# Grouping value sums by three, differencing sorted values where they are sorted, and moving six small operations to GpSimd in a graph network kernel

## The chip, the cores and the metric

The kernel runs on one core of a Trainium2 chip. The metric is the device time of one execution in microseconds (us), the median of several runs. A difference counts if it is larger than about 0.2 per cent.

## What is computed

The input is 16 graphs of N = 1024 nodes with C = 64 features, a dense adjacency matrix for each, and a node mask. Four layers follow one another, each with a residual and a layer norm. Nearly all of the work is in the first layer, cut here to what matters:

```
adj_d = dilate(adj, mask)            # per node: m neighbours; if m > 10, remove every
                                     # ceil(m/2)-th neighbour, then make it symmetric
sv   = sort(x[neighbours of i])      # per node i and channel c
agg  = 0.25*q(0.25) + 0.5*q(0.5) + 0.25*q(0.75)    # quantiles, each interpolated
                                     # between two order statistics, lo and hi
y    = (relu((x + agg) @ W1 + b1) @ W2 + b2) * mask
```

Three quantiles with two order statistics each make S = 6 statistics. The other layers are three graph convolutions with the adjacency, one with a degree norm, and one weighted mean.

## The kernel before

The kernel does not sort per node. It sorts each channel of a graph once over all 1024 nodes (`sort_pair`, two graphs at a time, 128 rows of 1024 values), and then finds, for every node, the block of the sorted order in which its order statistic lies by counting neighbours with matmuls. The sort is a bitonic network on VectorE (called `V`, DVE in the profile) of 55 steps; what was swapped is written to device memory (`swaps`) and read back in 55 further steps that carry ranks back to the original order (tiles `sr`). Sorted values are in 64 blocks of F = 16.

The value of an order statistic is a sum of differences of sorted values, taken with matmuls, so the kernel needs second differences along the sorted order, split in two fp16 parts, in a tile `txw` with the block index on the partitions. Before the change `sort_pair` writes the sorted values in fp32 to device memory (`xs`, L404: 4 DMAs for each pair of graphs, runs of 16 values), and `steps_of` (L463 to L494), once for each graph, reads them back block by block (L476, L477), forms the differences on VectorE (tile `xc`), and writes `txw`, with zeros in the lanes of the other channel of a pair (factors `PEVEN`, `PODD`).

The main loop works on units: a graph, a group of channels (8 for each graph) and a half of the nodes, 16 units for each graph and 256 in all. Each unit has 6 places y, one for each statistic s, so there are 1536 values of y. At each y the program issues, with a lag: `words` (matmuls to `pw`), `ranks` (`pr_`), `steps` (`pv`, which reads `mt` and `txw`, then ScalarE's eviction to `val`) and `sums` (`fc`), then on VectorE `masks` for statistic y + 1 (a comparison `mt` and a product `pr`), and the counting matmuls `x` of the next unit, whose results ScalarE (`A`, ACT in the profile) evicts to `cc` and `dw`.

`sums` takes the fp32 tiles `val` of two statistics at every second place and multiplies each by the constant `fin`. Each result has 32 rows, and the statistic number modulo 3 selects the group of 32 columns of the array and of 32 partitions of the bank `fc`:

```
for i in (s - 1, s):
    g3, second = i % 3, i // 3
```

Work for other graphs is put between: the sort of the next pair, the dilation of the next graph (`dilate`), the degrees, and the last three layers of the graph before (`layers`). They are Python generators; a class `Spread` steps them at places (two places for each y) so that they are spread evenly to a due place, and holds them back where a simple count of VectorE's work (2.9 us allowed for each place) says that it is behind. A generator may ask for a pause: `yield "4"` is at least four places. All orders are fixed when the program is built: each engine runs its own instructions in that order, and nearly every DMA is issued by SyncE's queue (SP), also in order. Tiles come from pools with a fixed number of buffers; `mt` has four, `pr` two, `cc` and `dw` two, `val` three, and the sort's tiles (tag `s`, names `sv`, `sr`, `ii`) two. `layers` calls a power on GpSimd (POOL) for `rstd` (L774), the only GpSimd work in the loop beside the index ramp `ii` (L412).

In `dilate`, for each of 8 row tiles t of a graph, VectorE makes a running count (`TENSOR_TENSOR_SCAN`) and then six operations on one number for each node (tile `sk`, L532 to L539); after a pause ScalarE uses them as a bias (L543), and VectorE goes on.

Ahead of the loop the first pair is sorted and the first graph dilated, one dilation step for every four sort steps (L1096).

Of the kernel before, what the change touches and what calls it, by code (L numbers as in the profile page):

```python
# [10 lines left out]
F32 = mybir.dt.float32  # L11
F16 = mybir.dt.float16
# [5 lines left out]
ALU = mybir.AluOpType  # L18
AX = mybir.AxisListType

P = 128
T_THRESH = 10.0

MAGIC = 1.5 * 2.0**23
EPS = 1e-5

TURN = 2
# [10 lines left out]
def gnn_stack(  # L38
# [220 lines left out]
    nc.sync.dma_start(out=mask8, in_=maskT)  # L259


    rows_in = [dram1.tile([5, C, N], F16, name=f"rows{i}") for i in range(2 * TURN)]


# [94 lines left out]
    def sort_pair(b, rows, found):  # L359
# [33 lines left out]
        V.tensor_scalar(  # L393
            scaled, v, lo, bits[:, 1:2].bitcast(F32), ALU.subtract, ALU.mult
        )
        v = scaled
        back = dram.tile([P, 2], F32, name="back")
        nc.sync.dma_start(out=back, in_=t[:, 0:2])
        xs = dram.tile([TURN, C // 2, P, F], F32, name="xs")
        for u in range(TURN):  # L400
            for c2 in range(2):
                q0 = (u * 2 + c2) * (C // 2)

                nc.sync.dma_start(  # L404
                    out=xs[u].rearrange("q (b c) f -> c q b f", c=2)[c2],
                    in_=v[q0 : q0 + C // 2, :].rearrange("q (b f) -> q b f", f=F),
                )
        found.append((xs, back))
        yield
        ii, _, _ = slot("ii")  # L410
# [49 lines left out]
                in_=rows.rearrange("y (c q) n -> q y c n", c=2)[KC * gr + k],  # L460
            )

    def steps_of(xs, back, found):  # L463

        least = small.tile([P, 2], F32, tag="least", name="least", bufs=3)
        txw = graph.tile([P, C // 2, 2, 2, F], F16, tag="txw", name="txw", bufs=2)
        found.update(least=least, txw=txw)  # L470
        for h in range(2):
            nc.sync.dma_start(out=least[h * C : (h + 1) * C], in_=back)
        xc = dil.tile([P, 2 * N], F16, tag="d", name="xc").bitcast(F32)
        cur = xc[:, 0:512].rearrange("p (q f) -> p q f", f=F)
        prev = xc[:, 512:1024].rearrange("p (q f) -> p q f", f=F)
        nc.sync.dma_start(out=cur, in_=xs.rearrange("q p f -> p q f"))  # L476
        nc.sync.dma_start(out=prev[2:P], in_=xs[:, 0 : P - 2, :].rearrange("q p f -> p q f"))  # L477
        yield
        V.tensor_copy(prev[0:2], cur[0:2, :, 0:1].to_broadcast([2, C // 2, F]))
        V.tensor_tensor(cur, cur, prev, ALU.subtract)  # L480
        yield

        tx = prev
        V.tensor_tensor(tx[:, :, 0 : F - 1], cur[:, :, 1:F], cur[:, :, 0 : F - 1], ALU.subtract)
        V.tensor_copy(tx[:, :, F - 1 : F], cur[:, :, 0:1])
        part = xc[:, 0:256].bitcast(F16).rearrange("p (q f) -> p q f", f=F)
        yield
        for i in range(2):
            V.tensor_copy(part, tx)
            V.tensor_scalar(txw[:, :, i, 0, :], part, PEVEN, None, ALU.mult)  # L490
            V.tensor_scalar(txw[:, :, i, 1, :], part, PODD, None, ALU.mult)
            if i < 1:
                V.tensor_tensor(tx, tx, part, ALU.subtract)
            yield  # L494


    def dilate(g, found):

# [14 lines left out]
        for t in range(T):  # L513
            sc = dil.tile([P, 2 * N], F16, tag="d", name="sc")
            nb, cum = sc[:, 0:N], sc[:, N : 2 * N]
            q = vt[:, t, :]
            for h in range(2):
                V.tensor_scalar(nb[:, ts(h, HALF)], a[h], 0.0, None, ALU.is_gt)
                A.activation(
                    q[:, ts(h, HALF)], a[h], AF.Copy, accum_out=den[:, h, t : t + 1]  # L520
                )
            if t + 1 < T:
                a = block_of(t + 1)
            V.tensor_tensor(nb[:, ts(t, P)], nb[:, ts(t, P)], offdiag, ALU.mult)

            V.tensor_tensor_scan(cum, nb, nb, 0.0, ALU.add, ALU.max)
            yield
            m = cum[:, N - 1 : N]


            sk = small.tile([P, 5], F32, tag="sk", name="sk")
            V.tensor_scalar(sk[:, 0:1], m, 0.5, 0.5, ALU.add, ALU.mult)  # L532
            V.tensor_scalar(sk[:, 0:1], sk[:, 0:1], MAGIC, -MAGIC, ALU.add, ALU.add)
            V.tensor_scalar(sk[:, 1:2], m, T_THRESH, mk[:, t : t + 1], ALU.is_gt, ALU.mult)
            V.scalar_tensor_tensor(
                sk[:, 2:3], sk[:, 0:1], 1.0, sk[:, 1:2], ALU.add, ALU.mult
            )
            V.tensor_scalar(sk[:, 3:4], sk[:, 2:3], -1.5, 1.5, ALU.mult, ALU.add)
            V.tensor_scalar(sk[:, 4:5], sk[:, 2:3], 0.5, -0.5, ALU.mult, ALU.add)  # L539
            yield "4"  # L540

            for h in range(2):
                A.activation(  # L543
                    q[:, ts(h, HALF)], cum[:, ts(h, HALF)], AF.Abs, bias=sk[:, 3:4]
                )
                yield "2"
            V.tensor_scalar(q, q, sk[:, 4:5], 0.25, ALU.is_equal, ALU.max)
            V.tensor_tensor(q, q, nb, ALU.mult)
            V.scalar_tensor_tensor(
                q[:, ts(t, P)], ident16, 0.25, q[:, ts(t, P)], ALU.mult, ALU.add  # L550
            )
            yield
# [117 lines left out]
    class Unit:  # L670
# [43 lines left out]
        def steps(self, s):  # L714

            pv, mt, nt = bank(ps_e, "pv"), self.mt.pop(s), self.nt.pop(s)
            for i in range(2):
                for k, o in quarters(pv):
                    mm(o, self.gi["txw"][:, KC * self.gr + k, i], mt[:, k], i == 0, False, k)
            for k, o in quarters(pv):  # L720
                mm(o, nbig[:, 32 * k : 32 * k + 32], nt, False, True, k)
            val = work.tile([P, HALF], F32, tag="val", name="val", bufs=3)
            A.activation(val, pv, AF.Relu)
            self.val[s] = val

        def sums(self, s):

            if s == 1:
                self.fc = bank(ps_f, "fc")
            for i in (s - 1, s):  # L730
                g3, second = i % 3, i // 3
                f0 = 16 - 16 * second
                mm(
                    self.fc[32 * g3 : 32 * g3 + 32], fin[:, f0 : f0 + 32], self.val.pop(i),
                    not second, bool(second), g3,
                )

        def weigh(self):
# [237 lines left out]
    def sort_of(i, found):  # L976
        return sort_pair(i * TURN, [rows_of(i * TURN + u) for u in range(TURN)], found)

    def all_of(gen):
        for _ in gen:  # L980
            pass
# [71 lines left out]

    def info(g):


        vt, rd, wd, den = parts.pop()
        infos[g] = dict(vt=vt, rd=rd, wd=wd, den=den, rB={})
        xs, back = sorted_[g // TURN]
        u = g % TURN  # L1060
        return steps_of(xs[u], back[u * C : (u + 1) * C], infos[g])

    def units():
        for g in range(B):
# [25 lines left out]
    for i, _ in enumerate(sorting):  # L1090
        if i == 0:
            onerow = strm.tile([P, N], F32, tag="a", name="onerow").bitcast(F16)[0:C, 0:N]
            V.memset(onerow, 1.0)
            for r in rows_in:
                nc.sync.dma_start(out=r[4], in_=onerow)
        if i % 4 == 3:  # L1096
            next(dilating, None)
    load_rows(rows_of(0), 0)
    load_rows(rows_of(0), 1)
# [7 lines left out]
                word_end(words[0][k], part // 2)  # L1107
            next(dilating, None)
    all_of(dilating)
    stepping = info(0)  # L1110
    next(stepping)
    for s in range(S):
        load_rank(0, s)

# [23 lines left out]
    _, counting = unit_of(0)  # L1138
    all_of(counting)
    live[0].masks(0)  # L1140
    all_of(stepping)

# [40 lines left out]
    for y in range(n_units * S + S):  # L1185
# [4 lines left out]
        if running and z == 0:  # L1190
            infos[g]["aggd"] = dram.tile([C, N], F32, name="aggd")
            deg = small.tile([P, 3, T], F32, tag="deg", name="deg")
            base = 2 * SLOTS * g
            if g == 0 and TURN < B:
                background.append(
                    Spread(sort_of(1, sorted_), 2 * n_sort + 6, 0, base + 2 * SLOTS + ROWS)
                )
            if g + 1 < B:
                background.append(Spread(dilate(g + 1, parts), 64, base, base + 168))
            background.append(  # L1200
                Spread(degrees(g, deg), 2 * T + 2, base, base + 184)
            )
            infos[g]["deg"] = deg
# [3 lines left out]
            if 0 <= v < n_units:  # L1207
                getattr(live[v], what)(s)
        v, s = divmod(y - 4, S)
        if 0 <= v < n_units and s % 2:  # L1210
            live[v].sums(s)
        v, s = divmod(y - 6, S)
        if 0 <= v < n_units and s == S - 1 and all_units[v][2]:
# [19 lines left out]
        for half in range(2):  # L1233

            if running:
# [3 lines left out]
                if g % TURN and place == base + ROWS and g + 3 < B:  # L1239

                    background.append(
                        Spread(
                            sort_of((g + 3) // TURN, sorted_), 2 * n_sort + 6, place,
                            place + 4 * SLOTS,
                        )
                    )
# [1 line left out]
                for b in sorted(background, key=lambda b: -b.late(place)):  # L1248
                    b.at(place)
                if z == 84 and half and g + 1 < B:  # L1250
                    background.append(Spread(info(g + 1), 6, place + 1, base + 2 * SLOTS - 2))
            if running:
                words_at(2 * y + half)
            if nu < n_units:
# [66 lines left out]
```

## Time and profile before

| quantity | value |
|---|---|
| runs, median of 3 (lowest to highest) | 9365.63 us (9364.59 to 9366.08) |
| profiled execution, time | 9361.04 us |
| profiled execution, span | 9359.3 us |
| mean granted TensorE clock | 0.994 |
| TensorE busy | 8767.8 us |
| VectorE busy | 8314.5 us |
| ScalarE busy | 7189.3 us |
| GpSimd busy | 232.7 us |
| first `mt` of the loop starts | about 344 us |
| last matmul of `fc` | about 9220 us |

Busy time is the union of the spans of an engine's instructions. In the groups of the profile each line names the code line, the engine, the operation, out<-in by the program's names and the count; after the bar stand busy time and the mean of one in ns; after the second bar the idle time of the engine just before, and what ended it. L278 and L297 are helpers that record every matmul and every operation of VectorE and ScalarE, so groups are told apart by their tiles.

### The profile page before, as it was taken

Reading aid. Unit: us, or ns where it says so; the run is one execution under the profiler, and the core shown is the slowest. Engines: PE = TensorE matmul, PEld = TensorE weight load, DVE = VectorE, ACT = ScalarE, POOL = GpSimd, SP = SyncE. Lnnn points to the kernel's source line nnn. Section 1 sums busy time; section 2 is a strip of 40 time slices with the busy share of each in tenths; the row PEclk is TensorE's granted clock in tenths of the full one; section 3 lists DMA queues with packets and bytes.
Section 4 is the critical chain, followed back from the end, with each engine's and each line's share of the span. In section 5 each row is a group of like instructions: output and inputs, shape, how many; then the busy total and the mean of one; then the engine's idle time right before and its main releaser. Section 6 shows DMA issues by size and latency. Waiting matters only on the chain.

```text
span 9359.3 us, 188142 instructions
## 1 busy us (share of the span) xinstructions
PE 8767.8 (94%) x78785; PEld 3749.0 (40%) x78785; DVE 8314.5 (89%) x9681; ACT 7189.3 (77%) x12465; POOL 232.7 (2%) x155
## 2 busy tenths in 40 slices
PE   0699999999999999999999999999999999999997
PEld 0334444444444444444444444444444444444442
DVE  8799989999899998989899998999989999777663
ACT  0588878788787887878788787887878788787773
POOL 0000000000000000000000000000000000000000
PEclk9999999999999999999999999999999999999998
DMA  3111221222222222222222222222222222212111
GB/s 84 51 40 42 77 91 61 87 65 90 77 77 73 77 71 80 85 81 67 80 63 89 80 76 81 69 75 77 91 76 75 72 76 74 69 65 66 43 60 57
DMA packets 593540, 676.21 MB, mean 72 GB/s; under 512 B 298736, under 2 KB 413552, under 8 KB 592688
## 3 DMA queue, kind: packets, MB, share of 16 engines
q1 hardware_dynamic: 592688, 664.19, 22.6%
q8 instruction: 616, 10.09, 0.4%
q14 instruction: 236, 1.93, 0.1%
HBM read 584.29 MB, written 79.70 MB: 71 GB/s over the span
## 4 chain that ended last, share of the span: by engine, by line
PE 67%; DVE 20%; ACT 7%; issue 5%; DMA 1%; POOL 0%; SPq 0%; DVEq 0%; POOLq 0%; ACTq 0%
PE x L278 29%; PE pw L278 10%; PE pa L278 10%; PE pv L278 7%; DVE pr L297 5%; PE fc L278 5%; DVE mt L297 4%; DVE sv L297 2%; DVE sr L297 2%; ACT dw L297 2%; DVE vt L297 1%; DVE m L297 1%; PE pc L278 1%; ACT xw L297 1%; PE p L278 1%
## 5 line engine op out<-in xcount | busy, mean ns | idle before, releaser
L278 PE MATMUL x<-vt,xw 128*128 128x512 f16 x16384 | 3974.0, 380 | 91.8 <-ACT dw L297 73.8
L297 DVE TENSOR_TENSOR pr<-mt,dw 128x4096 f16<-128x4096 f16 x1536 | 3520.4, 2292 | 71.8 <-ACT dw L297 1.0
L297 DVE TENSOR_TENSOR mt<-cc,rB 128x2048 f16<-128x2048 f16 x1536 | 1871.8, 1219 | 667.7 <-PE pv L278 646.0
L278 PEld LDWEIGHTS <-xw 128*128 128x128 f16 x16384 | 1497.3, 98 | 1767.8 <-issue 450.5
L297 ACT ACTIVATE qq<-pw,col,icol 128x512 f16<-128x512 f32 x1536 | 1203.0, 783 | 783.0 <-PE pw L278 768.1
L297 ACT ACTIVATE xw<-pa 128x512 f16<-128x512 f32 x2048 | 1234.6, 603 | 450.5 <-PE pa L278 442.8
L297 ACT ACTIVATE dw<-x 128x512 f16<-128x512 f32 x2048 | 1115.8, 600 | 273.7 <-PE x L278 269.3
L278 PE MATMUL pa<-words_by,prow 128*128 128x128 f16 x8192 | 804.3, 221 | 313.7 <-DMA prow<-rows 272.3
L297 ACT ACTIVATE xw<-xw 128x1024 f16<-128x1024 f16 x1024 | 1085.3, 1060 | 11.2
L278 PEld LDWEIGHTS <-prow 128*128 128x128 f16 x8192 | 557.0, 98 | 1159.2 <-issue 961.0
L278 PE MATMUL pw<-pr,red 128*32 128x512 f16 x12288 | 930.4, 379 | 33.1 <-DVE pr L297 32.6
L297 ACT ACTIVATE val<-pv 128x512 f32<-128x512 f32 x1536 | 926.5, 603 | 6.8 <-PE x L278 3.3
L278 PE MATMUL pv<-mt,txw 128*32 128x512 f16 x12288 | 930.6, 379 | 0.2 <-ACT nt L297 0.2
L278 PE MATMUL fc<-val,fin 128*32 128x512 f32 x3072 | 789.0, 592 | 0.5 <-ACT val L297 0.5
L297 ACT ACTIVATE cc<-x 128x512 f16<-128x512 f32 x1024 | 610.3, 596 | 131.4 <-PE x L278 125.9
L297 DVE TENSOR_TENSOR sr<-sr 128x512 f16<-128x512 f16 x1336 | 600.4, 478 | 17.5
L278 PE MATMUL pw<-rB,subr 128*32 128x512 f16 x6144 | 615.6, 390 | 0.2
L278 PE MATMUL pv<-nt,nbig 128*32 128x512 f16 x6144 | 598.7, 379 | 0.0
L297 DVE TENSOR_TENSOR sv<-sv 128x512 f32<-128x512 f32 x880 | 566.7, 685 | 0.0
L278 PEld LDWEIGHTS <-txw 128*32 128x32 f16 x12288 | 330.0, 97 | 334.4 <-issue 1.9
L278 PEld LDWEIGHTS <-subr 128*32 128x32 f16 x6144 | 158.2, 92 | 676.3 <-issue 674.2
L774 POOL TENSOR_TENSOR rstd<-var,neghalf 128x8 f32<-128x8 f32 x112 | 222.2, 1984 | 8112.3 <-DVE var L297 8112.3
(3287 smaller groups left out, 7718.4 us busy)
## 6 DMA issues: line engine op xcount, KB each, us to landing
a<-adj_dram SPq DMA_DIRECT2D x360, 512.0 KB
a<-adjT_dram SPq DMA_DIRECT2D x240, 512.0 KB
da<-adj_dram SPq DMA_DIRECT2D x256, 256.0 KB
ac<-adjT_dram SPq DMA_DIRECT2D x256, 256.0 KB
swaps<-m SPq DMA_DIRECT2D x440, 128.0 KB
m<-swaps SPq DMA_DIRECT2D x440, 128.0 KB
rB<-rd SPq DMA_DIRECT2D x96, 256.0 KB
prow<-rows SPq DMA_DIRECT2D x512, 20.0 KB
```

The source lines that it names most:

```text
L278: link("PE", nc.tensor.matmul(*args, **kw))
L297: ins = call(*args, **kw)
L774: nc.gpsimd.tensor_tensor(rstd, var, neghalf, ALU.pow)
```

## The change

There are three parts, and what follows from them.

**Sums.** `sums` runs at every third statistic, for three statistics at once, one in each of the three column groups. `val` gets a fourth buffer.

**Differences.** `sort_pair` forms the second differences itself, in the sort's own layout (first the difference from the same position of the block before, F values back, then that of neighbours); it splits them in two fp16 parts in the tile `both` and writes them with 8 DMAs for each pair of graphs, runs of 16 fp16 values, to `steps_in`, two buffers in device memory that were filled with zeros at the start. `steps_of` goes; `info` issues one DMA that reads a graph's `txw` whole, and the two for `least`. The sort has two more yields, and its due count is raised by two.

**Node figures.** The six operations on `sk` are issued on GpSimd, and one of them is now a `tensor_scalar` of two scalar operands.

Ahead of the loop, the dilation steps go between the second 55 steps of the first sort, one for every two.

```
+    steps_in = [dram1.tile([TURN, P, C // 2, 2, 2, F], F16, name=f"steps{i}") for i in range(2)]
...
-        xs = dram.tile([TURN, C // 2, P, F], F32, name="xs")
+        yield
+
+        down, _, _ = slot("sv")
+        V.tensor_copy(down[:, 0:F], scaled[:, 0:F])
+        V.tensor_tensor(down[:, F:N], scaled[:, F:N], scaled[:, 0 : N - F], ALU.subtract)
+        step, _, _ = slot("sv")
+        V.tensor_tensor(step[:, 0 : N - 1], down[:, 1:N], down[:, 0 : N - 1], ALU.subtract)
+        firsts, lasts = (a.rearrange("p (b f) -> p b f", f=F) for a in (down, step))
+        V.tensor_copy(lasts[:, :, F - 1 : F], firsts[:, :, 0:1])
+        yield
+        both = sorts.tile([P, 2 * N], F16, tag="s", name="sv")
+        V.tensor_copy(both[:, 0:N], step)
+        V.tensor_tensor(both[:, N : 2 * N], step, both[:, 0:N], ALU.subtract)
+        xs = steps_in[b // TURN % 2]
         for u in range(TURN):
             for c2 in range(2):
                 q0 = (u * 2 + c2) * (C // 2)
-                nc.sync.dma_start(
-                    out=xs[u].rearrange("q (b c) f -> c q b f", c=2)[c2],
-                    in_=v[q0 : q0 + C // 2, :].rearrange("q (b f) -> q b f", f=F),
-                )
+                for i in range(2):
+                    nc.sync.dma_start(
+                        out=xs[u].rearrange("(b e) q i c f -> e i c q b f", e=2)[c2, i, c2],
+                        in_=both[q0 : q0 + C // 2, ts(i, N)].rearrange("q (b f) -> q b f", f=F),
+                    )
...
-    def steps_of(xs, back, found):
...
             sk = small.tile([P, 5], F32, tag="sk", name="sk")
-            V.tensor_scalar(sk[:, 0:1], m, 0.5, 0.5, ALU.add, ALU.mult)
...
-            V.scalar_tensor_tensor(
-                sk[:, 2:3], sk[:, 0:1], 1.0, sk[:, 1:2], ALU.add, ALU.mult
-            )
...
+            G = nc.gpsimd
+            G.tensor_scalar(sk[:, 0:1], m, 0.5, 0.5, ALU.add, ALU.mult)
+            G.tensor_scalar(sk[:, 0:1], sk[:, 0:1], MAGIC, -MAGIC, ALU.add, ALU.add)
+            G.tensor_scalar(sk[:, 1:2], m, T_THRESH, mk[:, t : t + 1], ALU.is_gt, ALU.mult)
+            G.tensor_scalar(sk[:, 2:3], sk[:, 0:1], 1.0, sk[:, 1:2], ALU.add, ALU.mult)
+            G.tensor_scalar(sk[:, 3:4], sk[:, 2:3], -1.5, 1.5, ALU.mult, ALU.add)
+            G.tensor_scalar(sk[:, 4:5], sk[:, 2:3], 0.5, -0.5, ALU.mult, ALU.add)
...
-            val = work.tile([P, HALF], F32, tag="val", name="val", bufs=3)
+            val = work.tile([P, HALF], F32, tag="val", name="val", bufs=4)
...
-            if s == 1:
+            if s == 2:
                 self.fc = bank(ps_f, "fc")
-            for i in (s - 1, s):
-                g3, second = i % 3, i // 3
-                f0 = 16 - 16 * second
+            second = s // 3
+            f0 = 16 - 16 * second
+            for g3 in range(3):
                 mm(
-                    self.fc[32 * g3 : 32 * g3 + 32], fin[:, f0 : f0 + 32], self.val.pop(i),
-                    not second, bool(second), g3,
+                    self.fc[32 * g3 : 32 * g3 + 32], fin[:, f0 : f0 + 32],
+                    self.val.pop(3 * second + g3), not second, bool(second), g3,
                 )
...
+        least = small.tile([P, 2], F32, tag="least", name="least", bufs=3)
+        for h in range(2):
+            nc.sync.dma_start(out=least[h * C : (h + 1) * C], in_=back[u * C : (u + 1) * C])
+        txw = graph.tile([P, C // 2, 2, 2, F], F16, tag="txw", name="txw", bufs=2)
+        nc.sync.dma_start(
+            out=txw.rearrange("p q i c f -> p (q i c f)"),
+            in_=xs[u].rearrange("p q i c f -> p (q i c f)"),
+        )
...
+            nothing = strm.tile([P, N], F32, tag="a", name="nothing").bitcast(F16)
+            V.memset(nothing, 0.0)
+            for r in steps_in:
+                for u in range(TURN):
+                    nc.sync.dma_start(
+                        out=r[u].rearrange("p q i c f -> p (q i c f)"), in_=nothing
+                    )
-        if i % 4 == 3:
+        if i > n_sort and i % 2:
             next(dilating, None)
...
-    stepping = info(0)
-    next(stepping)
+    info(0)
...
-    all_of(stepping)
...
-        if 0 <= v < n_units and s % 2:
+        if 0 <= v < n_units and s % 3 == 2:
             live[v].sums(s)
...
-                    background.append(Spread(info(g + 1), 6, place + 1, base + 2 * SLOTS - 2))
+                    info(g + 1)
```

More of the change, by code (lines that the diff above doesn't have):

```diff
@@ L395, in sort_pair @@
         )
-        v = scaled
         back = dram.tile([P, 2], F32, name="back")
         nc.sync.dma_start(out=back, in_=t[:, 0:2])
-        xs = dram.tile([TURN, C // 2, P, F], F32, name="xs")
+        yield
[11 more added lines that the diff above has]
+        xs = steps_in[b // TURN % 2]
         for u in range(TURN):
@@ L461, in load_rows @@
             )
-    def steps_of(xs, back, found):
[L468 to L494, printed above, removed]
     def dilate(g, found):
@@ L531, in dilate @@
             sk = small.tile([P, 5], F32, tag="sk", name="sk")
-            V.tensor_scalar(sk[:, 0:1], m, 0.5, 0.5, ALU.add, ALU.mult)
-            V.tensor_scalar(sk[:, 0:1], sk[:, 0:1], MAGIC, -MAGIC, ALU.add, ALU.add)
-            V.tensor_scalar(sk[:, 1:2], m, T_THRESH, mk[:, t : t + 1], ALU.is_gt, ALU.mult)
-            V.scalar_tensor_tensor(
-                sk[:, 2:3], sk[:, 0:1], 1.0, sk[:, 1:2], ALU.add, ALU.mult
-            )
-            V.tensor_scalar(sk[:, 3:4], sk[:, 2:3], -1.5, 1.5, ALU.mult, ALU.add)
-            V.tensor_scalar(sk[:, 4:5], sk[:, 2:3], 0.5, -0.5, ALU.mult, ALU.add)
+            G = nc.gpsimd
[5 more added lines that the diff above has]
+            G.tensor_scalar(sk[:, 4:5], sk[:, 2:3], 0.5, -0.5, ALU.mult, ALU.add)
             yield "4"
@@ L1060, in info @@
         u = g % TURN
-        return steps_of(xs[u], back[u * C : (u + 1) * C], infos[g])
+        least = small.tile([P, 2], F32, tag="least", name="least", bufs=3)
[6 more added lines that the diff above has]
+        )
+        infos[g].update(least=least, txw=txw)
     def units():
@@ L1195, in gnn_stack @@
                 background.append(
-                    Spread(sort_of(1, sorted_), 2 * n_sort + 6, 0, base + 2 * SLOTS + ROWS)
+                    Spread(sort_of(1, sorted_), 2 * n_sort + 8, 0, base + 2 * SLOTS + ROWS)
                 )
@@ L1242, in gnn_stack @@
                         Spread(
-                            sort_of((g + 3) // TURN, sorted_), 2 * n_sort + 6, place,
+                            sort_of((g + 3) // TURN, sorted_), 2 * n_sort + 8, place,
                             place + 4 * SLOTS,
```

## The prediction

> **What bounds the kernel now.** I read the engines' shares first, then the chain that ended last, then the groups, then a table of stretches. The first two, from the page:
>
> ```profile
> PE 8767.8 (94%) x78785; PEld 3749.0 (40%) x78785; DVE 8314.5 (89%) x9681; ACT 7189.3 (77%) x12465; POOL 232.7 (2%) x155
> PE 67%; DVE 20%; ACT 7%; issue 5%; DMA 1%; POOL 0%; SPq 0%; DVEq 0%; POOLq 0%; ACTq 0%
> ```
>
> TensorE and VectorE are both nearly full and the chain passes from one to the other. The groups say how they are tied:
>
> ```profile
> L297 DVE TENSOR_TENSOR mt<-cc,rB 128x2048 f16<-128x2048 f16 x1536 | 1871.8, 1219 | 667.7 <-PE pv L278 646.0
> ...
> L278 PE MATMUL fc<-val,fin 128*32 128x512 f32 x3072 | 789.0, 592 | 0.5 <-ACT val L297 0.5
> ```
>
> VectorE waits almost only for `pv`, that is for one of the four `mt` buffers to come free: where it waits, TensorE is the bound. Which one binds where is seen in one graph, cut into eight stretches of 12 places (columns: window, its length, busy us of each engine, clock, DMA):
>
> ```profile
> 2547.00:2610.00 63.00, 61.76 (x588) 25.73 (x576) 62.04 (x71) 54.84 (x97) 0.00 (x0) 1.00 0.13 38
> 2610.00:2678.00 68.00, 62.41 (x549) 27.45 (x547) 66.79 (x76) 54.84 (x99) 2.48 (x1) 0.97 0.13 44
> ...
> 2892.00:2959.00 67.00, 65.53 (x634) 30.25 (x634) 64.72 (x68) 54.76 (x93) 4.22 (x2) 1.00 0.08 27
> 2959.00:3034.00 75.00, 74.17 (x706) 32.43 (x703) 62.44 (x80) 55.14 (x92) 2.62 (x2) 1.00 0.39 99
> ```
>
> In the first two VectorE (third pair) is full and never waits for `pv`; in the second, TensorE is idle for 5.6 us of 68. In the seventh and eighth VectorE is idle for 12.6 and 8.1 us (13.1 of it for `pv`) and TensorE for about 1 each: TensorE binds. The four between are close, TensorE a little ahead (11.1 us of waits for `pv` in 281 us). So a quarter of a graph is VectorE's, a quarter clearly TensorE's, half both.
>
> **What the Trainium skill says.** (1) "TensorEngine Tiling (Array Packing)", Key Properties: tiles of the array run independently, in parallel. "TensorE: Matmul & The Clock Gate", Why this matters for your kernels, gives 2.38 times for three column tiles. The trace agrees for two fp32 tiles and for four fp16 ones (below); it has no three. (2) "SBUF — State Buffer", Who interferes with whom: a GpSimd instruction that reads SBUF and a VectorE one with two SBUF inputs shut each other out. The trace shows half of that: `rstd` begun during an `mt` lasts till 1.5 us after its end (2.48 us against 1.64), while a `pr` that starts during `rstd` still takes 2.29 us. (3) "DMA: Bandwidth & Descriptors", Why a DMA increments its semaphore by 16 and not by 1: one descriptor for each contiguous run. So runs of half the size in twice the DMAs are twice the descriptors; see the sort below.
>
> **Sums.** The timeline of one place with sums:
>
> ```profile
> 4006.70 0.39 PE L278 MATMUL pv<-nt,nbig 128*32 128x512 f16 x4
> 4006.92 1.02 PE L278 MATMUL fc<-val,fin 128*32 128x512 f32 x4
> 4007.87 0.40 PE L278 MATMUL pa<-words_by,prow 128*128 128x128 f16 x4
> ```
>
> Each fp32 product is two passes. Inside the group (single records) both tiles' first passes start at 4006.92 and both second ones at 4007.35, 0.43 us apart: two statistics cost what one would, 0.86 us. The four `pv` start together too and take 0.22 us. From the last `fc` pass to `pa` there is 0.1 us more, as after `pv` where no sums follow (0.32 instead of 0.22), so that stays. A unit has three pairs now and two triples then: one slot of 0.857 us less in each of 256 units, **219 us of TensorE**. The wait is unchanged: sums still follow the eviction of `val` by one place. `val` 0 is held two places longer, which the fourth buffer covers.
>
> **VectorE.** The six `sk` operations: 47.2 + 26.1 + 20.4 + 18.7 = 112 us. `steps_of`, groups `xc` and `txw`: 22.0 + 19.7 + 13.4 + 10.4 + 6.5 + 3.1 = 75 us. Added for each of 8 sorts: two fp32 differences of some 1010 values, about 1.2 us each (0.685 for 512), a mixed one of 1.2, a cast of 0.69 (that of `ii`), two small copies of 0.35 together: 4.6, so 37 us. Net **150 us less**, of which 7 us a graph (`sk`) lie in the first five stretches, 0.13 us a place, just what TensorE loses a place (219/1536 = 0.143).
>
> So in the first five stretches both engines get lighter by 0.13 a place: 60 x 0.13 = 7.8 us. In the sixth VectorE has nothing less and only 2.3 us to spare: I take 1.2. In the last two TensorE binds: 24 x 0.143 = 3.4. Together 12.4 us a graph, x16 = **198 us gained**. `steps_of` ran in the eighth stretch, beside VectorE's idle time; I count nothing for it there.
>
> **The sort's new transfer.** Before:
>
> ```profile
> L297 DVE CAST sr<-ii 128x1024 f16<-128x1024 int32 x8 | 5.5, 694 | 23.8 <-DMA xs<-sv 23.8
> L404 SPq DMA_DIRECT2D xs<-sv x32: 625/1243/4350, 141.1 to 7427.5; - x32
> ```
>
> The cast needs the sort tile that the DMAs read, with two buffers then as now. Four DMAs of 2048 runs took 8.9 us from the first issue to the cast in the sort at 812 and 11.8 in that at 1849; the step before it hides most, and 14 of the 23.8 us are spread over six sorts in the loop. Eight DMAs of 2048 runs: if runs set the pace, 18 to 24 us, and VectorE waits 9 to 12 us more for each of seven sorts in the loop; if bytes do, as before. I take runs. The sorts come at 71 to 72 places of 96, so TensorE goes on for about one place (5.8 us) with what is ready, and VectorE's idle time in the seventh stretch pays the rest back: I charge 4 us each. SP is held as long, 16 us and more for 5 to 8; queued behind are `a` (L802, three buffers), `prow` and the sort's `m`. At 1857.6 `a` went out behind `xs` and TensorE waited 0.6 us for it; I charge 2 us. Seven sorts x 6 = **42 us lost** (0 to 90). The differences themselves, 4.6 us at the same spot, go under the seventh stretch's idle time; without it they cost 32.
>
> **GpSimd.** The price of a small `tensor_scalar` there is not in the trace. Below: 0.13 us (the ramp of 128x1). Above: `rstd`, mean 1.98. I take 0.2 plus a wait for the VectorE operation under way, about 0.8 each, 5 us for six. From the end of the count to ScalarE's use of `sk` there are 12.8 us in the loop (median; lowest 5.9, from the starts and ends of `TENSOR_TENSOR_SCAN` and `vt<-sc,sk`), so ScalarE rarely waits. Queued behind are `rstd` and then VectorE's scaling by it, and `ii`. VectorE may also wait for GpSimd's port, 0 to 0.2 us x 768. I charge **10 us** for all (0 to 150).
>
> **Start and end.** 2 MB of zeros leave by SP behind the first sort step, in front of `swaps`, whose two `m` buffers make VectorE wait: 3 to 6 us at the speed of the `da` loads, and 1 us for the fill. The first sort's transfer is bare: its wait was 9.4 us, and grows by 8. Its differences add 4.6. Off the path come five or six sets of `sk` (0.9 us each, 5 us) and `steps_of` of graph 0 (4.7 us of VectorE at 348 us, with two DMAs). The two last row tiles, in the open, pay a GpSimd round trip in place of VectorE's, 2 us each. Moving the dilation changes no sum; its `da` loads now stand before the `m` loads on SP: 0 to 5. Net **8 us lost** (-5 to 25). After 9220 us nothing changes.
>
> **Sum**: -198 + 42 + 10 + 8 = -138. The profiled execution took 9361.0 us (span 9359.3), 4.6 less than the median: 9223 against it, 9228 as a median. I give 9230.
>
> **Rivals.** (a) *VectorE takes over.* With port waits of 0.2 us x 768 eating its saving and late transfers in full (7 x 12), only the TensorE stretches gain: 16 x 5 - 60 = 20 to 60 us, about 9320. For it: VectorE's 2 us of slack in three stretches; against: `pr` was not slowed by `rstd`. (b) *The transfer costs nothing*, bytes setting the pace: 9155 to 9180. For it: TensorE's buffers; against: 64-byte runs already took 9 us for 0.5 MB. (c) *ScalarE stalls behind GpSimd*, slower. ScalarE runs in order; if six operations outlast the 12.8 us, each first use of `sk` holds the evictions `qq`, `nt`, `cc`, `dw` behind it, and TensorE runs out of banks. Each us late costs 128 us, so the gain is gone at 1.1 us late: a chain of 14 us, 2.3 us an operation. At 2.6 it is 2.8 us late: +358 - 138, about 9580. Against: `rstd` with its power is below that, and ScalarE has 22% idle. (d) *Three fp32 tiles don't run side by side* and a triple takes two slots: four slots for three, +219 TensorE, about 9500; against: four `pv` streams do.
>
> **Chances.** Forecast 0.60, (b) 0.15, (a) 0.15, (c) 0.06, (d) 0.02, the rest elsewhere. The range 9150 to 9325 takes in the forecast with its bounds, (b) and most of (a); (c) and (d) are left out. A measurement here tells about 0.2%, 19 us. Faster by more 0.88, within 0.03, slower 0.09.
>
> **What would show it.** Right: the `fc` group keeps its 3072 matmuls, but six passes in 0.86 us, at two places of six; `sk` in GpSimd's groups at 0.2 to 1 us each; `vt<-sc,sk` waiting little for it; the cast `sr<-ii` waiting some 10 us a sort for `sv`; the idle time of `mt` for `pv` about as now. The forecast is wrong if `fc` starts one tile later than its neighbours, if ScalarE's wait for `sk` in the loop passes 100 us, or if TensorE waits for `a` by tens of us.

## The result, and the profile after

The changed kernel takes 9304.6 us (9298.0 to 9308.0, four runs) against 9365.1 (the kernel before, now with a fourth run): a ratio of 0.9934, 95% interval 0.9917 to 0.9952. It is 60 us faster, where 138 were forecast. The profiled execution took 9303.8 us with a span of 9302.0.

The page of the kernel after, engines and chain:

```profile
PE 8584.0 (92%) x78785; PEld 3692.7 (40%) x78785; DVE 8194.6 (88%) x8786; ACT 7165.3 (77%) x12465; POOL 1064.4 (11%) x923
PE 62%; DVE 22%; ACT 7%; issue 7%; DMA 1%; POOL 1%; SPq 1%; another core or an unknown queue 0%; DVEq 0%; POOLq 0%; ACTq 0%
```

TensorE's busy time fell by 184 us and VectorE's by 120, but the span by only 57: most of what the engines were spared turned into idle time. The two groups, from the same page:

```profile
L299 DVE TENSOR_TENSOR mt<-cc,rB 128x2048 f16<-128x2048 f16 x1536 | 1871.6, 1218 | 677.4 <-PE pv L280 651.3
...
L280 PE MATMUL fc<-val,fin 128*32 128x512 f32 x3072 | 528.0, 593 | 0.0
```

The same 3072 products take 528 us in place of 789: a third is gone. The timeline shows three statistics in the time of one (start, us, then the instructions; `x6` is three products of two passes):

```profile
2994.89 0.39 PE L280 MATMUL pv<-nt,nbig 128*32 128x512 f16 x4
2995.11 1.03 PE L280 MATMUL fc<-val,fin 128*32 128x512 f32 x6
2996.07 0.62 PE L277 MATMUL pq<-ident,vt 128*128 128x128 f16 x8
```

Until the next matmul starts 0.96 us pass, as for two statistics before (0.95).

Where the time went is seen in the lengths of graphs, from a graph's first `mt` to the next one's. Of graphs 2 to 13, the odd ones fell from 557.5 us to 550.1 in the mean, the even ones rose from 558.1 to 559.9. The stretches of graph 4, as before the change (columns: window, length, busy of TensorE, its weight loads, VectorE, ScalarE, GpSimd, clock, DMA):

```profile
2536.00:2600.00 64.00, 61.69 (x598) 26.19 (x599) 62.30 (x67) 55.63 (x99) 8.91 (x6) 1.00 0.23 48
2600.00:2667.00 67.00, 61.37 (x553) 26.96 (x549) 66.25 (x66) 55.43 (x100) 20.24 (x13) 0.97 0.14 45
...
2877.00:2944.00 67.00, 64.71 (x634) 29.61 (x631) 65.02 (x74) 54.71 (x94) 2.32 (x2) 1.00 0.10 31
2944.00:3027.00 83.00, 74.02 (x697) 32.48 (x695) 63.08 (x72) 55.48 (x92) 2.62 (x2) 0.94 0.34 77
```

The first stretches are as long as before (64 and 67 us against 63 and 68), and VectorE is still full in them, though the figures `sk` are gone from it (what took their place is said below, with the differences). The seventh is 83 us in place of 75, with TensorE idle for 9 and a lower clock: that is where the sort's transfers are. Graph 5, with no sort there, has 72 us in that stretch.

Inside it the timeline gives the chain in four lines:

```profile
2959.57 11.28 SPq L419 DMA_DIRECT2D steps<-sv  x8
2974.77 0.69 DVE L299 CAST sr<-ii 128x1024 f16<-128x1024 int32 x1 [9.42 <-DMA steps<-sv]
2981.98 0.68 DVE L299 TENSOR_TENSOR msg<-pa,iv 128x512 f32<-128x512 f32 x1
2982.71 0.58 PE L277 MATMUL pq<-ident,vt 128*128 128x128 f16 x4 [7.73 <-DVE msg L299]
```

From the first of the eight issues to the cast that needs the tile 15.2 us pass; VectorE stands for 9.4 of them. Behind the cast, in VectorE's order, come seven more operations and then `msg`, which empties the one bank of the layers' chain; TensorE's next instruction is a transpose into that bank, and it stands 7.7 us. A table of stretches of 10 us shows the clock meanwhile:

```profile
2967.00:2977.00 10.00, 7.73 (x69) 2.85 (x62) 2.13 (x4) 6.29 (x11) 0.00 (x0) 1.00 0.79 149
2977.00:2987.00 10.00, 4.29 (x17) 2.10 (x17) 9.93 (x11) 1.20 (x2) 0.00 (x0) 0.50 0.21 73
```

The granted clock is 0.50 for these 10 us. TensorE stood from 2974.98 to 2982.71, so the clock fell some 2 us into the idle time and was full again 4.6 us after TensorE went on. (The Trainium skill, "TensorE: Matmul & The Clock Gate", Part 1: The HAM clock gate, says that a monitor sets the clock by how busy TensorE was lately; this trace agrees.) Only those 4.6 us of work ran at half clock, which costs 2.3 us by an estimate from these times.

Ahead of the loop, the first `mt` moved from 343.6 to 350.9 us, 7.3 later, where 8 were forecast.

### The profile page after: what moved, and what is told of

It reads as the page before. It is cut to its first block, busy times and chain, and to the rows that moved or that the text cites. A ratio compares the mean times of both kernels' runs of the same rounds, so it can differ in the third digit from the quotient of the medians.

```text
span 9302.0 us, 188268 instructions
## 1 busy us (share of the span) xinstructions
PE 8584.0 (92%) x78785; PEld 3692.7 (40%) x78785; DVE 8194.6 (88%) x8786; ACT 7165.3 (77%) x12465; POOL 1064.4 (11%) x923
## 4 chain that ended last, share of the span: by engine, by line
PE 62%; DVE 22%; ACT 7%; issue 7%; DMA 1%; POOL 1%; SPq 1%; another core or an unknown queue 0%; DVEq 0%; POOLq 0%; ACTq 0%
PE x L280 27%; PE pa L280 10%; PE pw L280 9%; PE pv L280 7%; DVE pr L299 6%; DVE mt L299 5%; PE fc L280 3%; DVE sr L299 3%; ACT dw L299 3%; DVE sv L299 2%; DVE vt L299 1%; PE p L280 1%; ACT xw L299 1%; DVE sc L299 1%; DVE m L299 1%
## 5 line engine op out<-in xcount | busy, mean ns | idle before, releaser
L299 DVE TENSOR_TENSOR pr<-mt,dw 128x4096 f16<-128x4096 f16 x1536 | 3520.5, 2292 | 72.5 <-ACT dw L299 1.0
L299 DVE TENSOR_TENSOR sv<-sv 128x512 f32<-128x512 f32 (+3 forms) x904 | 595.1, 698 | 0.6
L280 PE MATMUL fc<-val,fin 128*32 128x512 f32 x3072 | 528.0, 593 | 0.0
L515 POOL TENSOR_SCALAR sk<-sc 128x1 f32<-128x1 f16 x128 | 84.9, 663 | 3386.9 <-DVE sc L299 2310.7
```

Source lines behind the costliest of these rows:

```text
L280: link("PE", nc.tensor.matmul(*args, **kw))
L299: ins = call(*args, **kw)
L515: G.tensor_scalar(sk[:, 0:1], m, 0.5, 0.5, ALU.add, ALU.mult)
```

## The experiments

Twelve kernels ran. Times are medians; each ratio is to the kernel before on the same chip, with its 95% interval. "Part of the change" means that part of the diff shown above, put in or taken out as a whole. The kernel before took 9362.6 to 9368.3 us on these chips, so differences between kernels in us carry a few us of the chips. Lengths of graphs, waits and busy times come from one profiled execution of each kernel.

| kernel | time, us | ratio (95% interval) |
|---|---|---|
| sums by three alone | 9263.9 | 0.9894 (0.9879 to 0.9909) |
| sums, and `p8` first | 9263.8 | 0.9894 (0.9879 to 0.9909) |
| node figures on GpSimd alone | 9332.8 | 0.9968 (0.9955 to 0.9980) |
| differences alone | 9444.2 | 1.0087 (1.0072 to 1.0102) |
| after, with a pause | 9260.7 | 0.9893 (0.9878 to 0.9908) |
| sums and figures | 9237.1 | 0.9866 (0.9851 to 0.9880) |
| after, half the transfers | 9244.1 | 0.9876 (0.9859 to 0.9892) |
| after, figures on VectorE | 9346.8 | 0.9983 (0.9975 to 0.9990) |
| light before | 9259.8 | 0.9890 (0.9874 to 0.9907) |
| light, sums | 9139.7 | 0.9759 (0.9745 to 0.9774) |
| light, sums, `p8` first | 9114.0 | 0.9733 (0.9719 to 0.9748) |
| sums, figures, `p8` first | 9228.7 | 0.9849 (0.9832 to 0.9865) |

### The parts one by one

**Sums alone.** The edit is the first part of the change, put into the kernel before.

> The kernel before with the grouping of the sums by three as its only edit. Theory A (the sums save their 219 us of TensorE, but 128 times the products p8, which used to follow sums and now follow pv, wait for a bank, 0.37 us each, 47 us; and in the first two stretches of a graph VectorE is the bound and nothing is gained): 219 - 47 = 172, three quarters of it, 120 to 135 us less than before, about 9235. Rival B (the sums give less than the slot counted, the rest of the change gives the remainder): 40 to 70 us less, about 9310. Rival C (VectorE is the bound nearly everywhere, so that TensorE's saving needs VectorE's): under 30 us less.

99 us less. No reading had that: it lies between A and B. In this kernel's odd graphs the mean fell from 557.5 to 551.8 us, in graph 14, where no dilation or sort is left to do, from 552.5 to 541.8. So of the 13.7 us of a graph, 10.7 arrive where VectorE has little to do, and 5.7 where it is full.

**`p8` first.** What is new on TensorE is a wait. `total` puts two products `p8` (`p<-wv,fin` in the profile) in every twelfth place. Before, sums stood in that place between `pv` and `p8`; now they do not, and `p8` takes the bank of `pw` of the same place, which ScalarE is still emptying (`qq`). The groups of the kernel before and of the sums alone:

```profile
L278 PE MATMUL p<-wv,fin 96*32 96x512 f32 x512 | 133.3, 595 | 6.2 <-ACT qq L297 5.5 <-DVE wv L297 0.8
```
```profile
L278 PE MATMUL p<-wv,fin 96*32 96x512 f32 x512 | 135.7, 605 | 34.3 <-ACT qq L297 30.7 <-DVE wv L297 0.8
```

The edit moves four lines up, ahead of `words`:

```
+        v, s = divmod(y - 6, S)
+        if 0 <= v < n_units and s == S - 1 and all_units[v][2]:
+            total(...)
         for lag, what in ((1, "words"), (2, "ranks"), (3, "steps")):
...
-        v, s = divmod(y - 6, S)
-        if 0 <= v < n_units and s == S - 1 and all_units[v][2]:
-            total(...)
```

> As the kernel with the sums alone, and the products p8 are issued ahead of pw at the start of their place instead of behind pv. Theory A: their wait for the eviction qq goes, in the idle time before p<-wv some 30 us on TensorE and 40 us on its weight loads; 30 to 47 us less than with the sums alone. Rival (the wait is TensorE's slack: it is held by VectorE a little later in any case): within 15 us of the sums alone.

Nothing changed, 9263.8 against 9263.9, though the idle time before `p8` fell from 34.3 to 6.6 us. My expectation fell and the rival held: with VectorE at its full load, this wait taken off TensorE gains nothing. Only graphs 14 and 15 got shorter, by 1.7 and 0.9 us.

**Node figures alone.**

> The kernel before with the six node figures on GpSimd as its only edit; the dilation ahead of the loop stays where it was. Theory A (the figures take 6.6 us for six there, less than the 12.8 us that ScalarE leaves them, and VectorE's 112 us help only where it binds, a fifth to a quarter of the loop): 10 to 40 us less. Rival D (GpSimd keeps VectorE from its port or makes ScalarE and rstd late, which eats the gain of the other parts): 20 us slower or more. A third reading, 100 us less, would say that VectorE is the bound everywhere.

30 us less, as theory A had it; rival D falls. ScalarE waits for the figures 12 times in the loop, 13.8 us in all. VectorE's busy time fell from 8314.5 to 8226.1 us, by 88 where 112 had been counted from the means of the six operations. Three of the six groups of figures on GpSimd, in the kernel after:

```profile
L517 POOL TENSOR_SCALAR sk<-sc,mk 128x1 f32<-128x1 f16 x128 | 217.3, 1698 | 12.6
L518 POOL TENSOR_SCALAR sk<-sk 128x1 f32<-128x1 f32 x128 | 202.5, 1582 | 13.0
L515 POOL TENSOR_SCALAR sk<-sc 128x1 f32<-128x1 f16 x128 | 84.9, 663 | 3386.9 <-DVE sc L299 2310.7 <-ACT dw L299 549.1 <-ACT val L299 145.7
```

The means of all six add up to 6.6 us.

**Differences alone.**

> The kernel after with the sums in pairs and the node figures on VectorE: the differences in the sort's layout alone, with the dilation ahead of the loop in the second half of the sort. Theory A (VectorE waits 9.4 us for the eight transfers in each sort in the loop, TensorE waits for VectorE in the open layers' chain and runs at half clock for some us behind it, 8 to 9 us for each of seven sorts; 7 us more ahead of the loop; VectorE's saving lies where TensorE binds): 50 to 75 us slower than before, 9415 to 9440. Rival E (the even graphs lose for another reason, such as the sort's two more steps or GpSimd): within 20 us of before.

81 us more, a little above the expectation. The first `mt` comes at 353.0 us, 9.4 later than before, and the even graphs 2 to 12 take 568.4 us in the mean, the odd ones 3 to 13 558.8.

The kernel after set beside the kernel with sums and figures (below), which differ by this part alone, shows where it acts (means of graphs 2 to 13, between the starts of `mt` at every twelfth place). The last stretch, from which `steps_of` is gone, is 3.3 us shorter, but the first two together are 2.9 us longer, where VectorE is full and, in the second, more of the sort's steps now lie. These nearly cancel. What is left is the seventh stretch of the even graphs, 9.8 us longer.

### What costs in the differences

**A pause.** One line of `sort_pair`, behind the eight transfers:

```
         found.append((xs, back))
-        yield
+        yield "6"
```

> The kernel after, with six places of pause between the eight transfers of the sort and the cast that needs their tile. Theory A (VectorE's wait of 9.4 us for them is what the seven even graphs lose, 8 to 9 us each beside the odd ones, with the half clock behind it): the wait in the loop goes, even graphs take as long as odd ones, 45 to 63 us less than the kernel after, 9241 to 9260. Rival E (SP's queue, held for 16 us, or VectorE's added differences are what costs): within 15 us of the kernel after, with the even graphs as long as before.

44 us less than the kernel after (41 when each is set against the kernel before on its own chip), just short of theory A's 45 to 63. The even graphs come down from 559.9 to 553.7 us, near the odd ones with 552.1 (in an execution 11 us slower than this kernel's median). The waits of VectorE in the loop, the kernel after (two names for one wait: it is put down to the transfer that came last) and then this one (us in total, times, longest):

```profile
DVE sr L299 <- DMA ac<-adjT_dram: 37.7, 4, 9.5
DVE sr L299 <- DMA steps<-sv: 28.4, 3, 9.5
```
```profile
DVE sr L299 <- DMA steps<-sv: 0.7, 1, 0.7
```

66 us of waiting in seven sorts became 0.7. SP is held nearly as long as before (10.5 us from the first issue to the end of the last in graph 4, against 11.3), so rival E falls for these 44 us. The half clock is not what they were: up to 9100 us the clock's records have 92 us at 0.50 in this kernel and 89 in the kernel after. Some 24 us remain above the kernel with sums and figures. 10.5 of them lie ahead of the loop (first `mt` at 351.8 us against 341.3); the rest was not tracked down.

**Half the transfers.** `for i in range(2)` around the transfers becomes `range(1)`.

> The kernel after, with the four transfers of the second fp16 part left out (so the low parts of the differences are zero): 8192 runs of 32 bytes for each sort in place of 16384; VectorE's operations are the same. Theory A with the number of runs as the pace: the transfers take 7 to 8 us in place of 15, the cast waits 0 to 3 us in place of 9.4, and 40 to 60 us go. If the added operations on VectorE are what costs: within 15 us of the kernel after.

60 us less than the kernel after, at the upper edge of theory A; the waits in the loop:

```profile
DVE sr L299 <- DMA steps<-sv: 21.5, 7, 3.6
```

3.1 us for a sort in place of 9.4, while VectorE's added operations are all there. This kernel is also within 7 us of the kernel with sums and figures, so those operations cost little. Bytes halve here too, so three kernels are needed to tell runs from bytes. In graph 4, from the first issue to the cast, 8192 runs of 32 bytes take 8.2 us, 8192 runs of 64 bytes 9.5 (sums and figures; 11.7 in the kernel before), and 16384 runs of 32 bytes 15.2. Runs count for more than bytes; but the change also has twice the DMAs, eight in place of four, so runs and DMAs are not told apart.

### The sums and figures together, and each in the whole

> The kernel before with the sums by three and the node figures on GpSimd, and the differences as before. Alone they gave 99 and 30 us. Theory A (TensorE binds in three quarters of a graph, VectorE in the first quarter, so each part works in another stretch and the gains add up, with a little more since a lighter TensorE lets VectorE bind more often): 129 to 145 us less than before, 9218 to 9234. Rival (both gains lie in the same waits): about 100 less, 9263.

126 us less than before, just short of the range of theory A and far from the rival: the two gains add up (99 and 30). This is the change without its differences, and it beats the kernel after by 67 us (65 when each is set against the kernel before on its own chip).

> The kernel after with the node figures back on VectorE: sums and differences together. Theory A (the parts add up: 99 less and 81 more): 10 to 30 us less than before, 9333 to 9353; the figures on GpSimd are then worth 30 to 45 us in the whole. Rival D (GpSimd is what eats the gain in the whole, since its chain of 6.6 us meets rstd and ScalarE there): faster than the kernel after, below 9300.

16 us less than before, as theory A had it, so on top of the other two parts the figures on GpSimd are worth some 42 us. Rival D falls again.

### VectorE out of the way

The light kernels ask whether the sums' saving is short on TensorE or is kept back by VectorE. They leave out the carrying back of the ranks, so they show timing alone. The edit in the second half of `sort_pair`:

```
-            d = d2[:, 0:HALF]
...
-            V.tensor_tensor(h2, hi, dv, ALU.subtract)
+            V.tensor_copy(r2, r)
```

> The kernel before with VectorE made lighter: in the 55 steps that carry the ranks back, the four operations of a step (1.7 us) are one copy of the tile (0.42 us), so the ranks are not carried back and the counts are of other data; the transfers stay. This takes some 64 us of VectorE out of two graphs, nearly all of it in the odd ones. Both theories: the odd graphs 10 to 25 us shorter than before (557 us), the even ones by 0 to 6. It is the base for the two kernels beside it.

> The light kernel with the sums by three. Theory A (with the real VectorE load the sums keep only 6 to 7.5 of their 13.7 us a graph since VectorE binds at many places of every stretch): with VectorE out of the way the odd graphs gain 10 to 11 us over the light base, as graphs 14 and 15 did (10.7 and 12.4), and the even ones still 6 to 7. Rival F (the saving is short on TensorE itself, the slot is not 0.86 us or something new is put behind it): the odd graphs gain 6 to 7.5 here too.

> The light kernel with the sums by three and the products p8 first in their place. Where VectorE had its real load this gave nothing. Theory A (the wait of p8 for a bank is real on TensorE, 0.3 to 0.4 us eight times a graph, and counts only where TensorE binds): 1 to 3 us less in the odd graphs than the light kernel with the sums, nothing in the even ones. Rival (that wait never counts, its time is only moved to pv): no difference in either.

| mean of a graph, us | even 2 to 12 | odd 3 to 13 |
|---|---|---|
| before | 558.1 | 557.5 |
| sums alone | 551.8 | 551.8 |
| light before | 554.9 | 556.6 |
| light, sums | 549.1 | 547.3 |
| light, sums, `p8` first | 549.5 | 544.6 |

The light base is 104 us faster as a whole, but 72 of them lie ahead of the loop, where the first sort stands alone (first `mt` at 271.5 us against 343.6). I had expected it to be 10 to 25 us shorter in the odd graphs; it is 0.9, though VectorE's busy time is 51 us less in an odd graph (and 18 in an even one, all of it in the last two stretches). VectorE's relief went into waiting. The group of the light base, to be held against 646.0 us in the kernel before:

```profile
L297 DVE TENSOR_TENSOR mt<-cc,rB 128x2048 f16<-128x2048 f16 x1536 | 1873.1, 1219 | 1138.2 <-PE pv L278 1111.6 <-ACT cc L297 17.3 <-PE x L278 3.9
```

So in the odd graphs TensorE is only just the bound: with VectorE lighter alone 0.9 us go, with TensorE lighter alone 5.7, with both 10.2 (each to about 0.7, from the scatter of the six graphs). The sums gain 9.3 us an odd graph over the light base, near the 10 to 11 expected, and 5.8 an even one; rival F falls. And `p8` first, worth nothing at the real load, is worth 2.7 us in the odd graphs and nothing in the even ones, as theory A had it. Where VectorE is out of the way, 12.0 of the counted 13.7 us arrive: 9.8 of 10.3 in the first six stretches, which the light kernel relieves in an odd graph, and 2.2 of 3.4 in the last two, which it does not. The whole times agree: over the light base the sums save 120 us, and 146 with `p8` first, against 99 at the real load.

### The best version

> The kernel before with the sums by three, the node figures on GpSimd and the products p8 first in their place; the best that the runs point to. The two parts gave 126 us together; p8 first gave nothing with the full VectorE load, 2.7 us an odd graph (26 us in all) with the light one. The figures take only 7 us a graph off VectorE, of which little reaches the stretches where it binds, so the theory expects 0 to 12 us less than the sums with the figures, 9225 to 9237, most of it in graphs 14 and 15. If VectorE were clear of the bound now, about 25 less, 9212.

9228.7 us, ratio 0.9849, the fastest that ran with the whole computation, 1.5% under the kernel before. It is 8 us below sums and figures alone, but the two intervals overlap, so only its lead over the kernels before and after is sure. Of what was expected of graphs 14 and 15, graph 14 gave 3.1 us and graph 15 nothing.

## Why the prediction was right or wrong

138 us less were forecast and 60 came. For sums and figures 198 were forecast, or 188 with the charge for GpSimd; 126 came. For the differences and the start 50 were charged; they cost 67. Of the 78 us missing, some 62 are thus a gain sized too large, and the rest a cost sized too small. The measured time lies inside the stated range because that range took in most of rival (a), not because the sum was right.

**Right: the sums' slot.** Three fp32 products run side by side: 0.96 us to the next matmul for three, 0.95 for two. Rival (d) falls. TensorE's busy time fell by 184 us of the 219 counted (196 to 200 in the light kernels); why not by all of them was not tracked down.

**Wrong: what of it counts.** The step that failed is the sum "12.4 us a graph, x16 = 198 us gained". Sums and figures together gave 7.5 a graph. The terms, set against the lengths of stretches between the starts of `mt` (us saved in a graph, mean of graphs 2 to 13; the last two rows are of the odd ones alone):

| stretches | 1 and 2 | 3 to 5 | 6 | 7 and 8 | sum |
|---|---|---|---|---|---|
| forecast | 3.1 | 4.7 | 1.2 | 3.4 | 12.4 |
| sums alone | 0.3 | 4.1 | 0.3 | 1.3 | 6.0 |
| figures alone | 1.3 | 0.3 | -0.2 | 0.2 | 1.6 |
| both | 1.6 | 4.1 | 0.1 | 1.7 | 7.5 |
| light, sums | 3.1 | 3.4 | 1.7 | 1.1 | 9.3 |
| light, sums, `p8` first | 3.7 | 4.4 | 1.7 | 2.2 | 12.0 |

The differences from graph to graph leave about 0.6 us of doubt in the first two columns of "both", less in the others.

- Stretches 1 and 2: "in the first five stretches both engines get lighter by 0.13 a place". VectorE is the bound here, as the prediction had it; the sums alone give 0.3. But the 7 us of the figures were spread evenly over five stretches. VectorE's busy time fell by only 5.6 us a graph, and by 1.3 in these two, and that is about what the figures gave. With VectorE light, the sums give 3.1, and 3.7 with `p8` first: the whole slot of 3.4.
- Stretch 6: VectorE had "only 2.3 us to spare", and 1.2 were taken; 0.1 came. With VectorE light 1.7 arrive, the whole slot. So VectorE holds it, though its idle time in the stretch is larger than the saving.
- Stretches 7 and 8: "in the last two TensorE binds: 24 x 0.143", with "the wait is unchanged". Half came. The sums' own wait is unchanged, but I did not ask what the sums had stood in front of: without them in its place `p8` stands in the open. In the even graphs, where the light kernel takes 18 us off VectorE in just these stretches, the sums give 2.0 us in place of 1.2, and 2.6 with `p8` first. So VectorE and `p8` each have a part in it; the last 0.8 was not tracked down.

`p8` is no large part of the miss: at the real load putting it first gave nothing as a whole.

**Too small: the sort's transfer.** 42 us were charged for it and 8 for the start; the differences cost 67. The wait was sized a little large (9 to 12 us more; it went from 2.1 to 9.4 a sort in the loop, 7 more), and SP is held for 11 us where 16 and more were expected. The working behind "4 us each", that TensorE goes on for about one place and the seventh stretch pays the rest back, is what failed: TensorE stood 7.7 us at once behind the layers' bank, and the stretch grew by 9.8 us in the even graphs. "2 us" for `a` behind SP was too much: no wait of TensorE for `a` shows in the loop of the kernel after, and the 0.6 us that it rested on is a wait of the weight loads. The pause is worth 44 us, about what I charged for the whole transfer.

**Right: the start**, 7.3 us against 8 (9.4 with the differences alone). The first sort's bare transfer waits 14.4 us (from 9.4; 8 more were expected), and VectorE's waits for `swaps` grew from 3.6 to 7.1 us, with one of 4.05.

**GpSimd**: a charge of 10 us for which the runs show little. The chain takes 6.6 us against 5 estimated and hides in the pause; rival (c), the slower side, falls with ScalarE's 3.0 us of waiting in the loop of the kernel after. Of rival (a) the mechanism holds, VectorE taking over, but not its causes: `pr` still takes 2292 ns, so no cost of GpSimd to it shows. Rival (b) falls.

## What to carry to other kernels

When two engines are both near full, the relief of one is worth only its lead over the other, place by place; a table of stretches shows which leads in the mean, not at each place. Count a relief in the stretch where it lies, not spread evenly. Before pricing, make the second engine light and see what the first one's saving is worth. When work moves out of a place, ask what it stood in front of; and when a transfer reads a tile of a short pool, the next user of that tile needs a pause as long as the transfer, or what stands behind it in that engine's order pays.

## What was not expected of the hardware

GpSimd's operations on one number a partition stretch under VectorE's load. In the open, ahead of the loop (start, us):

```profile
306.49 0.19 POOL L515 TENSOR_SCALAR sk<-sc 128x1 f32<-128x1 f16 x1 [10.75 <-DVE sc L299]
306.78 0.30 POOL L517 TENSOR_SCALAR sk<-sc,mk 128x1 f32<-128x1 f16 x1
```

0.19 and 0.30 us, against means of 0.66 and 1.70 over the run. In the loop, the operation of L517 takes 0.48 us in the mean where no `mt` or `pr` runs beside it (28 times), and 2.18 where one does (92 times). The Trainium skill, "SBUF — State Buffer", Who interferes with whom, has each of the two engines shut out by the other; here the loss is GpSimd's alone: the 233 `pr` that meet an operation of GpSimd take 2292 ns in the mean, as do the 1303 that do not, and the 59 that start while one is under way take 2293.

TensorE's wait of 7.7 us behind the sort cost it a little more than its length, an estimated 2.3 us, since the clock stayed at half for 4.6 us of work after it. But time at half clock does not by itself measure a loss: up to 9100 us the clock's records have 27 us of it in the kernel before, 89 in the one after and 92 in the one with the pause, which is 44 us faster than the one after.
